# Four-wave fillers in the second attention, and sums of gelu outputs by accumulating DMAs

## The chip, the cores and the metric

The kernel runs on one core of one Trainium2 chip. The metric is device time in microseconds (us) of one execution. Three executions of the kernel before took 3659.13 us in the median (3658.23 to 3659.21).

The engines are named as in the profile: PE multiplies matrices, PEld loads its weights, DVE (vector engine) and ACT (scalar engine) work element by element and read PSUM, POOL (GpSimd) does small vector work and issues DMAs, and SP issues DMAs.

## The reference

The input x is 16 images of 256 channels by 32x32 pixels, so 1024 tokens of 256 channels for each image. Two layers follow one another, all in float32:

```
# layer 0: attention with 4 heads of 64, residual added to the tokens
qkv  = xs @ w_proj + b_proj
attn = softmax(q k^T * 64**-0.5);  res = (attn v) @ w_out + b_out + xs

# layer 1: group norm, attention with 8 heads of 32, then an MLP
x = x + attention(group_norm(x), qkv_w, proj_w, proj_b, phys_bias)
h = group_norm(x)
h = gelu(mlp_w1 h + mlp_b1)          # 256 -> 1024 channels
x = x + (mlp_w2 h + mlp_b2)          # 1024 -> 256 channels
```

## The kernel before

**Batches and stages.** The 16 images (batches b = 0 to 15) are a software pipeline. One pass of the loop runs attention_0 of batch b (L0's heads of 64, function `attention_a`), then the first half of the MLP of batch b-1 (`hidden`), then the q and k of layer 1 for batch b, then attention_1 of batch b (`attention_b`). Beside attention_1, PE also does the second half of the MLP of batch b-1 (`outputs`) and the q, k and v of layer 0 for batch b+1 (`first`): these are the fillers.

**attention_b.** Its work is cut into 16 units of two key blocks each, plus a last step, here called steps 0 to 16. In step n, PE computes the scores of unit n (`s_b`, L563, 32 matmul records), then the weighted values of unit n-1 (`acc_b`, L607, 16 records, always in PSUM bank 0), and then the fillers of this step. ACT takes the exponentials of the scores (`e_b`, L578). DVE sums the exponentials (`es_b`, L591) and adds the weighted values to the result (`res_b`, L620), or ACT copies them in steps 1, 5, 9 and 13 (L618). The first scores of the next step go to banks 0 and 1 and the rest to "wide" tiles. There are three wide tiles of two banks each, taken in turn, the one used longest ago first; a filler also takes a wide tile, unless a number in `aside` sends it to bank 0 or 1. A tile can be written again when its reader is done: so the scores of step n+1 wait for the L620 of step n and for the copies of its fillers.

**Denominators.** For b = 1 to 14, when a group of four units is complete, its summed exponentials are folded from 128 to 64 partitions by two DMAs (`fold`, L632 and L633): SP copies one half to `packed_b`, and POOL adds the other half with an accumulating DMA. Three ticks later PE sums the result (`den_b`, L642); the inverse then travels through DMAs of SP to `rd_b` and is multiplied in by DVE (L682).

**Fillers.** A q or k piece of layer 0 (`first[0]` to `first[7]`) is 16 records of 512 columns. A v piece, of layer 0 (`first[8]` to `first[11]`) or of layer 1 (`v[0]` to `v[3]`), is 32 records of 256 columns in 32-column form. An output piece (`reduce`) is 32 records of 512 columns. The list `fill` says after which step each one runs. In batches 1 to 14 the q and k of layer 1 come just before step 0 by `qk_by_seven`, 14 pieces in a chain of seven products for each half, and one v piece stands before the last of them. `weigh` of unit n needs `v[n]` (n = 0 to 3).

**The MLP by seven products.** Both halves of the MLP use seven products of half size in place of eight. In `mlp`, the 16 tiles of gelu outputs `gs` (128x512) are combined by sums and differences before the second half's products read them: first in `finish` (the call of `combine` with one index, minus), and later in `reduce`, where a product with a `then` entry calls `combine(*then, True)` for four tiles (L1112). The list `products` gives the order and the three `then` entries: after product 2, (0,0) += (1,1); after 3, (0,1) += (0,0); after 4, (1,0) += (0,0). Product 1 reads (0,0) after that, product 6 reads (0,1), product 7 reads (1,0). A product with two destinations copies its PSUM tile to `lent` on ACT, and its additions (L1171, and `then`) run one tick later.

**What sets the order.** The program is written as one stream. A planner puts it into one queue for each engine: it walks through a simulated time and gives an engine, among the instructions that are ready, the one that was written first. An instruction that is not ready yet is overtaken. `keep_in_program_order` ties an instruction behind the one written before it on its engine, as `add` does with all sums of exponentials but the first of a unit. `Later` holds callbacks that run after a number of ticks; a tick is run in every step before the fillers. At run time each engine executes its queue strictly in order, and waits on semaphores.

Of the kernel before, what the change touches and what calls it, by code (L numbers as in the profile page):

```python
# [11 lines left out]
ALU = mybir.AluOpType  # L12
# [247 lines left out]
def first_pass(ctx, tc, x, out, k):  # L260
    nc = tc.nc
    B, C, S = x.shape
# [25 lines left out]
    def load_blocks(m, b, at_end=False):  # L288
        if not at_end:
            t = act.tile([P, 7, TB], F32, tag="ws", name=f"w{m}_{b}")  # L290
            nc.sync.dma_start(t, kept_blocks[m])
            blocks[m] = [t[:, n] for n in range(7)]
            return
        one = act.tile([P, 4, TB], F32, tag="k0", name=f"w{m}_{b}_0")
        two = act.tile([P, 4, TB], F32, tag="x", name=f"w{m}_{b}_1", bufs=3)
        nc.sync.dma_start(one, kept_blocks[m][:, :4])
        nc.sync.dma_start(two[:, :3], kept_blocks[m][:, 4:])
        blocks[m] = [one[:, n] for n in range(4)] + [two[:, n] for n in range(3)]
# [11 lines left out]
    def wide(name, n=None):  # L310
        if n is None:
            n = next(m for m in order if m not in kept)
        use(n)
        return ps_s.tile([P, 2, TB], F32, tag=f"s{n}", name=name)

    def bank(name, n):
        return ps_a.tile([P, TB], F32, tag=f"b{n}", name=name)
# [12 lines left out]
    def load_x(b):  # L330
        t = act.tile([P, CC, S], F32, tag="x", name=f"x_{b}", bufs=3)
        n = S if b else TB
        for s0 in range(0, S, n):
            for cc in range(CC):
                nc.sync.dma_start(
                    t[:, cc, s0 : s0 + n], x[b, cc * P : (cc + 1) * P, s0 : s0 + n]
                )
        return t
# [15 lines left out]
    def product(o, w, r, **flags):  # L354
        for c0 in range(0, P, cols[0]):
            sl = slice(c0, c0 + cols[0])
            nc.tensor.matmul(o[sl], w[:, sl], r, **flags)  # L357
# [681 lines left out]
    def mlp(b, xb):  # L1039
        n4 = HC // 2  # L1040
        gs, open_sums = {}, {}
# [67 lines left out]
        def combine(to, what, plus, only=None):  # L1109
            for i in range(n4) if only is None else (only,):  # L1110
                d = gs[(*to, i)]
                (nc.vector.tensor_add if plus else nc.vector.tensor_sub)(  # L1112
                    d, d, gs[(*what, i)]
                )
# [17 lines left out]
        def reduce(number, right, outs, then):  # L1132
            ps = wide(f"m2_{b}_{number}")[:, 0, :]
            for i in range(n4):
                product(
                    ps, blocks[2][number - 1][:, i * P : (i + 1) * P], gs[(*right, i)],
                    start=(i == 0), stop=(i == n4 - 1),
                )
            bias, num = None, 1
            if len(outs) == 1:  # L1140
                bias = k["m2b2"]

                num = 2 if b == B - 1 and number == 7 else 1
            elif number in (2, 5):
                bias = k["m2b"]
            co = outs[0][0]
            if len(outs) == 2:

                if not lent:
                    lent.append(act.tile([P, 4, TB], F32, tag="v0", name=f"lent_{b}"))  # L1150
                m = lent[0][:, number % 4]
                if bias is not None:
                    nc.scalar.activation(m, ps, AF.Identity, bias=bias[:, co : co + 1])
                    bias = None
                else:
                    nc.scalar.copy(m, ps)
                ps = m

            def add_up():
                for co, t, plus in outs:  # L1160
                    missing[co, t] -= 1
                    n = TB // num
                    for u in range(num):
                        sl = slice(t * TB + u * n, t * TB + (u + 1) * n)
                        y, p = xb[:, co, sl], ps[:, u * n : (u + 1) * n]
                        if bias is not None:
                            nc.vector.scalar_tensor_tensor(
                                y, p, bias[:, co : co + 1], y, ALU.add, ALU.add
                            )
                        else:  # L1170
                            (nc.vector.tensor_add if plus else nc.vector.tensor_sub)(y, y, p)  # L1171
                        if not missing[co, t]:
                            nc.sync.dma_start(out[b, co * P : (co + 1) * P, sl], y)
                if then:
                    combine(*then, True)


            if len(outs) == 2 and b < B - 1:
                later.after(1, add_up)
            else:  # L1180
                add_up()
# [13 lines left out]
    def run_pieces(pieces, tick=True):  # L1195
        for piece in pieces:
            piece()
            if tick:
                later.tick()
# [14 lines left out]
    ps, n = bank("bqk", 0), brow.shape[0]  # L1214
# [10 lines left out]
    for m in (1, 2):  # L1225
        made = act.tile([P, 7, TB], F32, tag="ws", name=f"w{m}_made")
# [23 lines left out]
    for b in range(B):  # L1250
        def load_next(b=b):
            if not b:
                xs[1] = load_x(1)
                return
            with tc.issue_after(spread_out["last"].ins):
                load_blocks(1, b - 1)
                if b + 1 < B:
                    xs[b + 1] = load_x(b + 1)

        later.after(14, load_next)  # L1260
        xn = []
        seven = 0 < b < B - 1
        load_qk, sums_for_qk, qk_pieces = qk_by_seven(b)
        run(
            attention_0(
                b, tiles0, xs[b],
                lambda st, b=b, xn=xn, seven=seven, then=sums_for_qk: group_norm(
                    f"g{b}", xs[b], st, k["g1w"], k["g1b"], "res", xn, 2 if b else 3,
                    then if seven else None,
                ),  # L1270
            )
        )
        if seven:
            load_qk()
        first = []
        if b + 1 < B:
            tiles0, (first_qk, first_v) = qkv_0(b + 1, xs[b + 1])
            first = first_qk + first_v
        run_pieces(first if b == 0 else hidden)
        later.flush()  # L1280
        if b:
            load_blocks(2, b - 1)
        if b == B - 1:
            load_blocks(1, b, True)
        tiles1, (qk, v) = qkv_1(b, xn[0])
        n = len(qk) // CC

        if seven:  # L1290
            made = qk_pieces(*tiles1[:2])
            run_pieces(made[:-1] + v[:1] + made[-1:])
        else:
            aside.extend((1, 0))
            run_pieces(qk[:n] + v[:1])
        def early(piece):
            aside.append(0)
            piece()

        own = [lambda: early(v[1]), qk[n], v[2], qk[n + 1], v[3], *qk[n + 2 :]]  # L1300
        now, end = outputs, []
        if b == 0:
            first = []
        if b == B - 1:

            now, end = outputs[:3], outputs[3:]
        if not first:

            fill = {m: [piece] for m, piece in enumerate(own[:5:2] + own[1::2] + own[6:])}
            fill.update({len(own) + 3 * m: [piece] for m, piece in enumerate(now)})  # L1310
            now = []

        if first:
            o = [[piece] for piece in now]
            f = [first[1:2]] + [first[n : n + 2] for n in range(2, 10, 2)]
            fill = dict(enumerate((
                [own[0], v[2]], [v[3], first[0]],
                o[0], f[0], o[1], o[2], f[1], o[3], f[2], o[4], f[3], o[5], f[4], o[6],
                [], first[10:11],
            )))  # L1320
            fill[last + 1] = first[-1:]
        hn = []
        run(
            attention_1(
                b, tiles1, xs[b],
                lambda st, b=b, hn=hn: group_norm(
                    f"h{b}", xs[b], st, k["g2w"], k["g2b"], "q1", hn,
                    *((3 if b + 1 < B else 1), lambda y, b=b: sums_of_input(b, y)),
                ),
            ),  # L1330
            fill,
        )
        run_pieces(end)
        hidden, outputs = mlp(b, xs[b])
# [309 lines left out]
```

## Time and profile before

| | |
|---|---|
| time, median of 3 | 3659.13 us |
| time of the profiled execution | 3658.71 us |
| span of the profile | 3656.9 us |
| PE busy | 3620.8 us (99%) |
| DVE busy | 2739.4 us (75%) |
| ACT busy | 2140.2 us (59%) |
| POOL busy | 198.6 us (5%) |
| granted PE clock | 0.999 |
| DMA by POOL (queue q0) | 28.21 MB, 5.0% of the 16 DMA engines' span |

The span is what the profile covers; the execution's own time is 1.8 us longer. A busy share belongs to the whole span: PE at 99% says that PE has nearly always a matmul in it, not that it runs at its peak, since a matmul that waits behind another one counts as busy. So the profile is best read by steps: how long from one step's first score matmul to the next one's, and what that step had to do. In a timeline, the columns are start, duration, engine, line, operation, and in brackets the idle time of that engine before it and what ended it.

### The profile page before, as it was taken

The page shows a single profiled execution, that of the slowest core. Times are in us where ns is not written, and L with a number is a line of the kernel's source. Part 1 is how long each engine was busy: PE and PEld are TensorE (multiplying, and loading weights), DVE is VectorE, ACT ScalarE, POOL GpSimd, SP SyncE. Part 2 cuts the span into 40 slices and gives each one's busy share as a digit, 9 for nine tenths or more (in the row PEclk, how much of TensorE's full clock was granted, in tenths as well). Part 3 has the DMA queues.
Part 4 walks back from the last instruction along what each step waited for, and adds up shares of the span by engine and source line. Part 5 has one row for each costly group of instructions (what it writes and reads, how often), then busy time and mean ns, then how long its engine had stood idle before and what let it go on. Part 6 is the DMA issues. An engine that isn't in the chain of part 4 may idle for free.

```text
span 3656.9 us, 79215 instructions
## 1 busy us (share of the span) xinstructions
PE 3620.8 (99%) x33829; PEld 1352.0 (37%) x33829; DVE 2739.4 (75%) x3560; ACT 2140.2 (59%) x2861; POOL 198.6 (5%) x317
## 2 busy tenths in 40 slices
PE   9999999999999999999999999999999999999998
PEld 3433343333433334333343433434334343333433
DVE  5687777777777777877778777787777877777787
ACT  4665656556565655656556565565655656556572
POOL 4000000000000000000000000000000000000000
PEclk9999999999999999999999999999999999999999
DMA  3011211212121121211312112121221212203100
GB/s 122 10 54 38 58 60 38 66 41 75 41 47 57 41 77 39 51 59 36 77 39 54 56 46 67 39 54 56 53 60 39 54 56 53 66 33 63 52 26 26
DMA packets 81566, 190.28 MB, mean 52 GB/s; under 512 B 37974, under 2 KB 38742, under 8 KB 76982
## 3 DMA queue, kind: packets, MB, share of 16 engines
q1 hardware_dynamic: 71828, 156.53, 14.0%
q0 software_dynamic: 7632, 28.21, 5.0%
q8 instruction: 267, 4.37, 0.5%
q14 instruction: 93, 0.76, 0.1%
q10 hardware_dynamic: 1746, 0.40, 0.1%
HBM read 118.51 MB, written 21.75 MB: 38 GB/s over the span
## 4 chain that ended last, share of the span: by engine, by line
PE 82%; issue 10%; DVE 7%; ACT 1%; DMA 1%; POOL 0%; SPq 0%; ACTq 0%; DVEq 0%; POOLq 0%
PE s_b L563 13%; PE s_a L425 12%; PE acc_a L446 12%; PE acc_b L607 11%; PE m L357 9%; PE qk_a L357 5%; PE qk L972 3%; PE v_a L357 3%; PE v_b L357 3%; PE j L357 3%; PE m L1050 2%; PE o L357 2%; DVE es_b L591 2%; PE qk7y L972 1%; PE den_a L479 1%
## 5 line engine op out<-in xcount | busy, mean ns | idle before, releaser
L578 ACT ACTIVATE e_b<-s_b 128x1024 f32<-128x1024 f32 (+1 forms) x1280 | 982.6, 865 | 237.8 <-PE s_b L563 237.8
L591 DVE TENSOR_TENSOR es_b<-es_b,e_b 128x1024 f32<-128x1024 f32 x768 | 899.2, 1219 | 199.6 <-ACT e_b L578 198.3
L433 ACT ACTIVATE e_a<-s_a 128x1024 f32<-128x1024 f32 x512 | 520.8, 1024 | 360.2 <-PE s_a L425 343.6
L563 PE MATMUL s_b<-q,k 32*64 32x512 f32 x8192 | 543.4, 601 | 13.0 <-DVE res_b L620 10.7
L425 PE MATMUL s_a<-q,k 64*64 64x512 f32 x4096 | 544.3, 593 | 0.0
L446 PE MATMUL acc_a<-e_a,v 64*64 64x512 f32 x4096 | 540.1, 589 | 0.0
L460 DVE TENSOR_TENSOR es_a<-es_a,e_a 128x1024 f32<-128x1024 f32 x384 | 473.3, 1233 | 67.5 <-ACT e_a L433 48.0
L607 PE MATMUL acc_b<-e_b,v 128*32 128x512 f32 x4096 | 492.1, 598 | 0.0
L357 PE MATMUL m<-g,w 128*32 128x512 f32 (+1 forms) x3320 | 404.3, 592 | 0.0
L563 PEld LDWEIGHTS s_b<-q,k 32*64 32x64 f32 x8192 | 170.2, 130 | 359.9 <-issue 150.3
L446 PEld LDWEIGHTS acc_a<-e_a,v 64*64 64x64 f32 x4096 | 187.9, 133 | 251.5 <-issue 222.9
L425 PEld LDWEIGHTS s_a<-q,k 64*64 64x64 f32 x4096 | 175.9, 133 | 246.7 <-issue 212.6
L1050 PE MATMUL m<-gn_h,w 128*128 128x512 f32 x512 | 243.7, 604 | 6.0 <-DVE g L1076 3.4
L357 PE MATMUL qk_a<-x,wp 128*32 128x512 f32 (+1 forms) x1856 | 235.3, 593 | 3.7 <-ACT k L834 3.7
L607 PEld LDWEIGHTS acc_b<-e_b,v 128*32 128x32 f32 x4096 | 108.5, 109 | 351.5 <-ACT e_b L578 194.7
L357 PEld LDWEIGHTS m<-g,w 128*32 128x32 f32 (+1 forms) x3320 | 121.4, 112 | 262.3 <-issue 230.6
L1112 DVE TENSOR_TENSOR g<-g,g 128x512 f32<-128x512 f32 x320 | 206.7, 678 | 8.7 <-ACT g L1063 8.5
L620 DVE TENSOR_TENSOR res_b<-res_b,acc_b 128x512 f32<-128x512 f32 x192 | 130.7, 681 | 102.1 <-PE acc_b L607 102.1
L591 DVE TENSOR_TENSOR es_b<-e_b,e_b 128x1024 f32<-128x1024 f32 x128 | 150.7, 1218 | 64.4 <-ACT e_b L578 64.4
L1050 PE MATMUL m<-hs,w 128*128 128x512 f32 x384 | 177.9, 592 | 0.1
L460 DVE TENSOR_TENSOR es_a<-e_a,e_a 128x1024 f32<-128x1024 f32 x64 | 78.4, 1225 | 108.0 <-ACT e_a L433 107.9
L1063 ACT ACTIVATE g<-g,m1b 128x512 f32<-128x512 f32 x128 | 92.2, 723 | 109.1 <-DVE g L1092 82.1
(179 smaller groups left out, 3092.9 us busy)
## 6 DMA issues: line engine op xcount, KB each, us to landing
w<-w_kept SPq DMA_DIRECT2D x30, 1792.0 KB
packed_b<-es_b SPq DMA_DIRECT2D x42, 512.0 KB
packed_b<-es_b POOLq DMA_DIRECT2D x42, 512.0 KB, 6.5
d_a<-row_a SPq DMA_DIRECT2D x64, 256.0 KB
rd_b<-row_b SPq DMA_DIRECT2D x252, 64.0 KB
out_dram<-x SPq DMA_DIRECT2D x63, 256.0 KB
x<-in_x_dram SPq DMA_DIRECT2D x30, 512.0 KB
qk<-qk_kept SPq DMA_DIRECT2D x14, 512.0 KB
```

The lines of the kernel that those rows point to most:

```text
L357: nc.tensor.matmul(o[sl], w[:, sl], r, **flags)
L425: nc.tensor.matmul(s[h : h + HALF, g, :], kT[g * D : (g + 1) * D, c, kb * P + h : kb * P + h + HALF], qT[g * D : (g + 1) * D, c, t * TB : ...
L433: nc.scalar.activation(e, s, AF.Exp, scale=float(D) ** -0.5)
L446: nc.tensor.matmul(accs[i][h][g * D : (g + 1) * D, :], v[h * HALF : (h + 1) * HALF, kb, c * 2 + g], e[h * HALF : (h + 1) * HALF, g, :], st ...
L460: nc.vector.tensor_add(sums[i], held[i] if kb == 1 else sums[i], e)
L563: nc.tensor.matmul(outs[g][h : h + HALF, :], kT[g * D : (g + 1) * D, c, k0 : k0 + HALF], qT[g * D : (g + 1) * D, c, t * TB : (t + 1) * TB] ...
L578: nc.scalar.activation(to, s, AF.Exp, scale=float(D) ** -0.5)
L591: ins = nc.vector.tensor_add(d, es[n % 2] if kb == 0 else d, es[n])
L607: nc.tensor.matmul(acc[g * D : (g + 1) * D, :], v[:, kb + m, c * G + g], es[2 * m + g // 2][:, g % 2, :], start=(m == 0), stop=(m == 1),)
L972: nc.tensor.matmul(to, w, st[x], start=first, stop=True, skip_group_check=not first)
L1050: nc.tensor.matmul(ps, blocks[1][number - 1][:, i * P : (i + 1) * P], inputs[b][number], start=first, stop=True, skip_group_check=not first,)
L1112: (nc.vector.tensor_add if plus else nc.vector.tensor_sub)(d, d, gs[(*what, i)])
```

## The change

There are three edits.

1. In `reduce`, for all batches but the last, the later sums of gelu outputs are no longer DVE additions. For each of the four tiles POOL issues a DMA from one SBUF tile to the other with an accumulating add. The differences in `finish` stay on DVE, and the last batch keeps DVE for all.
2. Before attention_1 (batches 1 to 14), `v[0]` no longer stands before the last piece of the q and k chain; the chain runs without it. `v[0]` and `v[1]` are the fillers of step 0, `v[2]` and `v[3]` those of step 1.
3. The other fillers are dealt anew. Before, step 1 had `v[3]` and `first[0]`, step 3 had `first[1]` alone, and steps 6, 8, 10 and 12 had two pieces of `first` each. After, steps 3, 5, 7 and 9 have two each, step 12 has `first[8]` alone and step 15 has `first[9]` and `first[10]`. The output pieces move with them: before they were in steps 2, 4, 5, 7, 9, 11 and 13, after in 2, 4, 6, 8, 10, 11 and 13.

```diff
                         if not missing[co, t]:
                             nc.sync.dma_start(out[b, co * P : (co + 1) * P, sl], y)
-                if then:
+                if then and b < B - 1:
+                    for i in range(n4):
+                        to, what = (gs[(*g, i)] for g in then)
+                        nc.gpsimd.dma_start(to, what, accum_op=ALU.add)
+                elif then:
                     combine(*then, True)
...
         if seven:
             made = qk_pieces(*tiles1[:2])
-            run_pieces(made[:-1] + v[:1] + made[-1:])
+            run_pieces(made)
         else:
             aside.extend((1, 0))
             run_pieces(qk[:n] + v[:1])
...
         if first:
             o = [[piece] for piece in now]
-            f = [first[1:2]] + [first[n : n + 2] for n in range(2, 10, 2)]
+            f = [first[n : n + 2] for n in range(0, 8, 2)]
             fill = dict(enumerate((
-                [own[0], v[2]], [v[3], first[0]],
-                o[0], f[0], o[1], o[2], f[1], o[3], f[2], o[4], f[3], o[5], f[4], o[6],
-                [], first[10:11],
+                [v[0], own[0]], v[2:],
+                o[0], f[0], o[1], f[1], o[2], f[2], o[3], f[3], o[4], o[5], first[8:9], o[6],
+                [], first[9:11],
             )))
             fill[last + 1] = first[-1:]
```

`own[0]` is `early(v[1])`: `v[1]` with its PSUM tile in bank 0.

## The prediction

> **What bounds the kernel now.** I read the page first, then the waits, then the timeline of one attention_1 (batch 8, scores from 1905.46 us on) engine by engine. The page says who is full and what the replaced additions cost.
>
> ```profile
> PE 3620.8 (99%) x33829; PEld 1352.0 (37%) x33829; DVE 2739.4 (75%) x3560; ACT 2140.2 (59%) x2861; POOL 198.6 (5%) x317
> L1112 DVE TENSOR_TENSOR g<-g,g 128x512 f32<-128x512 f32 x320 | 206.7, 678 | 8.7 <-ACT g L1063 8.5
> ```
>
> PE is the bound, and it does the same matmuls before and after, so only time in which PE waits can be won. The 180 additions that leave DVE (12 for each of 15 batches) are 122 us of DVE time, and DVE time is worth nothing unless PE waits for it. The list of waits has one such row:
>
> ```profile
> PE s_b L563 <- DVE res_b L620: 10.7, 16, 0.9
> ```
>
> Sixteen waits, about one for each batch. The timeline of steps 2 to 4 shows where:
>
> ```profile
> 1925.34 1.97 PE L563 MATMUL s_b<-q,k 32*64 32x512 f32 x32
> 1926.06 0.68 DVE L1112 TENSOR_TENSOR g<-g,g 128x512 f32<-128x512 f32 x1
> 1928.47 1.22 DVE L591 TENSOR_TENSOR es_b<-es_b,e_b 128x1024 f32<-128x1024 f32 x1
> 1928.99 1.90 PE L357 MATMUL qk_a<-x,wp 128*32 128x512 f32 x16
> 1929.60 1.29 DVE L1112 TENSOR_TENSOR g<-g,g 128x512 f32<-128x512 f32 x2
> 1930.81 0.68 DVE L620 TENSOR_TENSOR res_b<-res_b,acc_b 128x512 f32<-128x512 f32 x1
> 1931.55 1.98 PE L563 MATMUL s_b<-q,k 32*64 32x512 f32 x32 [0.66 <-DVE res_b L620]
> ```
>
> Step 3 has a short filler (one q/k piece), and DVE is still at the four additions when the accumulator in bank 0 is ready at 1929; L620 comes at 1930.81, and the scores of step 4 wait for it. Step 3 takes 6.21 us. A step with two q/k pieces takes 7.19 us (step 8, 1960.75 to 1967.94), and a second piece is 1.72 us (3.55 for two less 1.83 for one), so step 3 should take 5.47: it loses 0.74 us.
>
> **The change part by part**, for one of the batches 1 to 14.
>
> *v[0] leaves the q/k chain.*
>
> ```profile
> 1901.82 1.12 PE L972 MATMUL qk<-gn_g,qk 128*128 128x512 f32 x2
> 1901.94 0.69 DVE L1002 TENSOR_TENSOR q<-qk7p,qk 128x512 f32<-128x512 f32 x1 [0.17 <-PE qk L972]
> 1902.78 1.89 PE L357 MATMUL v_b<-wq,gn_g 128*128 128x256 f32 x8
> 1904.51 1.02 PE L972 MATMUL qk<-gn_g,qk 128*128 128x512 f32 x2
> ```
>
> The piece takes 1.73 us (1902.78 to 1904.51), and hid the DVE addition that the last product must wait for. That addition ends at 1902.63, and PE is busy with the product before it until 1902.78, so the cover is not needed: -1.73. If the last product must wait for more, it is at most one such addition, +0.69.
>
> *Step 0* keeps two v pieces (v[0], v[1] for v[1], v[2]; 5.49 us): 0 on PE. What changes is the eviction: n = 0 is copied by DVE, not ACT, and the sums of exponentials of unit 0 are tied behind that copy. PE ends the piece at 1910.95; the copy of 0.69 us can start about 0.2 later (1904.71 after 1904.51) and end at 1911.84. ACT's copy of the same place ended at 1911.67 and cost nothing. In step 14 a tile that was released 0.93 us after the scores began cost 0.12; here it would be 0.89, so +0.05, between 0 and +0.7 (where the copy stands behind a DVE addition instead). The two sums start 2.2 us later; DVE is idle 2.57 us before step 2's sum, which takes that up.
>
> *Step 1*: two v pieces (3.59 us in step 0) for a v and a q/k piece (3.56): +0.03.
>
> *Step 3*: two q/k pieces, 7.19 for 6.21: +0.98. Without the additions DVE reaches L620 when bank 0 is ready, 0.25 us after the weighted values end, as in step 4 (1935.44), and three sums of 3.49 us follow. The 1.72 us of q/k work moved here is thus paid with 0.98: the stall of 0.74 goes.
>
> *Steps 5 to 10* swap outputs and q/k pieces of equal length (3.55 each): 0.
>
> *Steps 12 and 15*: one v piece moves from 12 to 15, -1.73 and +1.73. Step 12 becomes short, so I look for a new stall there.
>
> ```profile
> 1989.94 2.68 PE L563 MATMUL s_b<-q,k 32*64 32x512 f32 x32
> 1990.82 0.66 DVE L1167 SCALAR_TENSOR_TENSOR x<-m,m2b,x 128x512 f32<-128x512 f32 x1
> 1994.29 3.64 PE L357 MATMUL v_a<-wp,x 128*32 128x256 f32 x64
> 1994.54 0.69 DVE L620 TENSOR_TENSOR res_b<-res_b,acc_b 128x512 f32<-128x512 f32 x1 [3.06 <-PE acc_b L607]
> ```
>
> DVE is idle 3.06 us before L620 here and done with it at 1995.2; the shorter step lets the next scores start at 1996.1: no stall. The inverse denominators of L682 in step 13 come by DMAs issued until 2000.8, and in the last step such a row is multiplied in 1.7 us after its last issue, so they land by 2002.5; L682 would now stand at 2002.9: 0, at most +0.5. The first line also shows a loss that stays: 2.68 us for scores that take 1.97 elsewhere, since the output product's tile is released by L1167, which stands behind three sums of exponentials. No replaced addition is near it. The same holds for step 15 (2.91 us, released by L722).
>
> *The accumulating DMAs.* POOL and queue q0 carry one of this kind already, the fold.
>
> ```profile
> 1939.85 0.95 POOL L633 DMA_DIRECT2D packed_b<-es_b  x1 [52.60 <-PE s_b L563]
> ...
> 1949.57 0.62 PE L642 MATMUL den_b<-packed_b,folded 128*32 128x128 f32 x16
> ```
>
> And the answer on that line alone gives its issue time (min, median, max in ns) and its landing:
>
> ```profile
> L633 POOL DMA_DIRECT2D packed_b<-es_b x42: 918/933/1022, 359.9 to 3351.5; - x42
> ...
> DMA to landing us min/median/max: 6.1/6.5/8.1
> ```
>
> A set of four costs POOL 4 x 0.93 = 3.7 us, three sets 11 us in a batch; POOL is idle nearly all of this stage. Nothing shows a 256 KB accumulating DMA: one takes no more than the fold's 6.5 us for 512 KB, and if four ran one after another a set would take 26 us. From start to start POOL's issue spacing and half of the bytes suggest 10 to 12 us for a set; I take 12. Who waits: product 1 for the first set, product 6 for the second, product 7 for the third. The sets are released at the start of steps 3, 7 and 9 (after products 2, 3 and 4), and those products stand in steps 10, 11 and 13, so at least 4 steps of about 7.2 us, 28 us with the shorter step 12, lie between, above even 26: 0. Queued behind them on POOL stand additions into dsum and isum, which nobody on PE awaits, and the fold. The fold's sum lands about 1946.4 and is read at 1949.57, 3 us of slack in item 0 (its step 3 set is issued 10 us earlier) and 5.8 us in item 1. Cost 0, up to +5.5 in item 1 if the third set gets ahead of the fold on q0. SP's queue gets nothing new, and its packets share the 16 DMA engines, which q0 now holds 8% of the span longer (47 MB by the page's 28.21 MB for 5.0%).
>
> The row shows 0.92 to 1.02 us for POOL's issue in a stage in which DVE is busy most of the time. A rule speaks against this edit: the Trainium skill, page "SBUF — State Buffer", summary of rules for kernel authors, says not to hide a DMA issued from GpSimd under DVE work but to use the hardware path, since descriptors can't be written while DVE holds the shared port. By it each issue might wait for one DVE operation, which would add 12 times at most 1.2 us (estimate with this trace's longest sum), 15 us to POOL and still 0 to PE; by the row, 0.
>
> **The sum.** -1.73 + 0.05 + 0.03 + 0.98 + 0 + 0 = -0.67 us for each of 14 batches: -9.4. In batch 15, which keeps its fillers, DVE drops the same additions: step 8 waits 0.65 us for L620 behind them (3532.82), and 2.57 us of them stand in the chain to the last group norm at 3588.5 to 3591, of which PE idles 0.65: I take -1.5 of 0 to -3. Together -10.9. Against the profiled execution's 3658.71 this is 3647.8; the median stands 0.4 above it, so 3648.2.
>
> **The rivals.** A measurement of this kernel can tell about 0.2% (7.3 us) from no change.
>
> *Slower: v[0] is put on PE before v[1].* In step 0, v[0]'s wide tile is released by the third exponential, 2.25 us after ACT starts (1906.58), so at 1908.8; PE would be ready at 1907.36: 1.5 us in each batch, 21 us in all, 3669. It decides if PE's queue follows the written order. Against it: v[1] is ready first (bank 0, first exponential), and the queue does leave the written order (in the chain, the sixth products of both halves stand side by side, which are not written so).
>
> *Slower: the fold gets stuck.* If the third set is issued before the fold of item 1, den_b waits 5.5 us in 14 batches: +77, about 3725. It decides if SP's copy for that fold lands after product 4 ends: in the trace POOL waits for it until 1966.48, and product 4 would end 1.5 us later. Close, but the copy is the earlier.
>
> *No change: the gain is given back* by v[0]'s copy (+0.7) or the last product (+0.69) at their upper ends: +0.6 to +1.3 in each batch, 3656 to 3666. For it speaks that both margins are within 0.2 us.
>
> *More: the stalls of steps 12 and 15 go too*, 0.71 + 0.94 us in 14 batches, 3625. Against it: both stand behind sums of exponentials, not behind the additions.
>
> **How the numbers follow.** My forecast 0.62, v[0] first 0.11, fold stuck 0.07, given back 0.15, more 0.05. Faster by over 0.2%: the forecast and "more", less a little of the forecast that ends short, 0.64. Same: most of "given back" and that little, 0.17. Slower: 0.19. The forecast's own range is 3644 to 3652. The range that leaves out the stuck fold and "more" is 3642 to 3669.
>
> **What would show it.** The wait of s_b for L620 falls from 16 rows to few; step 3 takes 7.19 us with two q/k pieces; the q/k chain runs without a v piece or idle PE; the period of a batch falls from 225.7 us (scores of batch 8 to batch 9, 1905.46 to 2131.18) to about 225.0; L1112 has 140 instructions, and POOL 180 more DMAs; no PE or PEld wait for a DMA. A PE wait for v, for qk or for packed_b would make me wrong.

## The result and the profile after

The kernel after takes 3691.88 us in the median (3688.76 to 3692.72), beside 3658.76 us for the kernel before: ratio 1.0089, 95% interval 1.0072 to 1.0107. It is slower by about 33 us. The forecast was 3648.2 us and the range ended at 3669. The profiled execution took 3692.72 us, with a span of 3690.6 us (before 3656.9), at a granted PE clock of 0.998.

The page of the kernel after: PE is still the bound, with 23.2 us more of "busy" and 33.7 us more of span. DVE lost 98 us and POOL gained 143 us, as the edit says. PE has 336 records more (34165 beside 33829), though it does the same products: in the chain of q and k, `v[0]` was 8 records of 128 columns, as the line L357 shown in the prediction has it, and as a filler it is 32 of 32 columns, 24 more in each of 14 batches. The second line is DVE's wait for the rows of the inverse denominators before L682; before it was 27.6 us.

```profile
PE 3644.0 (99%) x34165; PEld 1349.6 (37%) x34165; DVE 2641.1 (72%) x3380; ACT 2143.3 (58%) x2861; POOL 341.8 (9%) x497
L682 DVE TENSOR_TENSOR res_b<-res_b,rd_b 128x512 f32<-128x512 f32 x64 | 44.2, 690 | 135.3 <-DMA rd_b<-row_b 135.2
```

The groups by line: the additions of gelu outputs on DVE fell from 320 to 140.

```profile
L1112 DVE TENSOR_TENSOR g<-g,g 128x512 f32<-128x512 f32 x140 | 92.2, 682 | 8.7 <-ACT g L1063 8.5
```

The waits of PE (what waited, on whom, us in total, times, longest). The row that the prediction rested on, 16 waits for L620, is down to one. But two rows of PE were not there before, one of them at the top:

```profile
PE v_b L357 <- ACT e_b L578: 16.8, 14, 1.2
...
PE s_b L563 <- DVE x L1167: 2.6, 6, 0.8
...
PE s_b L563 <- DVE res_b L620: 0.9, 1, 0.9
```

The steps say how much each part moved. The table has the mean length in us over batches 1 to 14 of each step (from its first score matmul to the next step's), and the median of the stretch from step 15 to the next batch's first scores. Steps that are not listed are the same in both, to 0.01.

| | step 0 | step 1 | step 3 | step 12 | step 14 | step 15 to next batch |
|---|---|---|---|---|---|---|
| before | 5.49 | 7.20 | 6.20 | 7.92 | 7.74 | 118.40 |
| after | 6.77 | 7.98 | 7.19 | 6.28 | 8.59 | 118.41 |
| predicted for after | 5.54 | 7.23 | 7.19 | 6.19 | 7.74 | 118.40 |

So steps 0, 1 and 14 cost 1.28 + 0.78 + 0.85 = 2.91 us more in a batch, where the prediction had 0.08, and 2.83 x 14 = 40 us is nearly all of the 43.7 us between forecast and result. Step 3 and the stretch to the next batch came out as predicted (one v piece left the chain of q and k, -1.73, and one came to step 15, +1.73), and step 12 within 0.1.

**Steps 0 and 1.** First the kernel before, batch 8, where v[1] stands first and v[2] second. The two pieces (x64) start 1.90 us after the first scores, without a wait, and the copy of v[1] ends at 1910.89, before the scores of step 1 start:

```profile
1907.36 3.66 PE L357 MATMUL v_b<-wq,gn_g 128*32 128x256 f32 x64
1910.26 0.63 ACT L851 COPY v<-v_b 128x512 f32<-128x512 f32 x1
1910.95 1.97 PE L563 MATMUL s_b<-q,k 32*64 32x512 f32 x32
```

And the kernel after, batch 8 (first scores at 1925.21):

```profile
1925.21 1.97 PE L563 MATMUL s_b<-q,k 32*64 32x512 f32 x32
1926.33 3.83 ACT L578 ACTIVATE e_b<-s_b 128x512 f32<-128x512 f32 x5 [0.43 <-PE s_b L563]
1928.38 3.66 PE L357 MATMUL v_b<-wq,gn_g 128*32 128x256 f32 x64 [1.20 <-ACT e_b L578]
1931.98 2.74 PE L563 MATMUL s_b<-q,k 32*64 32x512 f32 x32
1932.11 0.59 ACT L851 COPY v<-v_b 128x512 f32<-128x512 f32 x1 [1.95 <-PE v_b L357]
1932.75 0.27 PEld L563 LDWEIGHTS s_b<-q,k 32*64 32x64 f32 x16 [0.59 <-ACT v L851]
```

PE's queue keeps the written order, v[0] and then v[1]. v[0] goes to a wide tile, which the third exponential releases, so PE idles 1.20 us; v[1], whose bank 0 was free long before, stands behind it. And so v[1] ends late: its copy on ACT runs from 1932.11 to 1932.70, and the scores of step 1, which need bank 0, wait for it (2.74 us for scores that take 1.97). The Trainium skill, "TensorE: Matmul & The Clock Gate", "Step-by-step: what each phase is for", says that the engine pulls only weight loads ahead and that matmuls stay in program order; these rows agree, as 1.20 us of idle PE were not filled with v[1], which was free to run.

**Steps 12 to 14.** Before, L682 of step 13 did not wait, and the scores of step 14 took 2.09 us (batch 8):

```profile
2004.64 0.68 DVE L682 TENSOR_TENSOR res_b<-res_b,rd_b 128x512 f32<-128x512 f32 x1
2005.05 2.09 PE L563 MATMUL s_b<-q,k 32*64 32x512 f32 x32
```

After, step 12 is shorter by 1.64 us, nearly the 1.73 that was planned, and L682 of step 13 comes that much earlier:

```profile
2017.08 1.91 PE L357 MATMUL v_a<-wp,x 128*32 128x256 f32 x32
2019.47 4.00 SPq L400 DMA_DIRECT2D rd_b<-row_b  x4
2026.11 2.78 PE L563 MATMUL s_b<-q,k 32*64 32x512 f32 x32
2026.39 0.69 DVE L682 TENSOR_TENSOR res_b<-res_b,rd_b 128x512 f32<-128x512 f32 x1 [0.60 <-DMA rd_b<-row_b]
2027.00 0.74 DVE L1167 SCALAR_TENSOR_TENSOR x<-m,m2b,x 128x512 f32<-128x512 f32 x1
```

SP issues the rows of the inverse denominators until 2023.47; they are all there at 2026.39, 2.9 us later. L682 waits for them, L1167 stands behind L682 on DVE, and L1167 is what releases the output product's tile to the scores of step 14: 2.78 us of scores, and a step of 8.43 us in this batch (7.84 to 9.51 over the batches).

**The predicted parts that came true.** Steps 3 and 4: DVE is idle for 0.43 us until bank 0 is ready, L620 starts 0.25 us after PE has gone on to the filler, and the scores of the next step take their 1.97 us.

```profile
1949.05 1.92 PE L607 MATMUL acc_b<-e_b,v 128*32 128x512 f32 x16
1950.79 3.62 PE L357 MATMUL qk_a<-x,wp 128*32 128x512 f32 x32
1951.04 0.69 DVE L620 TENSOR_TENSOR res_b<-res_b,acc_b 128x512 f32<-128x512 f32 x1 [0.43 <-PE acc_b L607]
1954.34 1.97 PE L563 MATMUL s_b<-q,k 32*64 32x512 f32 x32
```

The chain of q and k runs without the v piece: the DVE addition ends at 1923.24, and the last products, which need it, start at 1923.30:

```profile
1921.49 1.88 PE L972 MATMUL qk<-qk7t,qk 128*128 128x512 f32 x4
1922.55 0.69 DVE L1002 TENSOR_TENSOR q<-qk7p,qk 128x512 f32<-128x512 f32 x1
1923.30 1.98 PE L972 MATMUL qk<-gn_g,qk 128*128 128x512 f32 x4
```

The accumulating DMAs, by the answer on their line alone (issue time on POOL in ns, minimum, median and maximum, and landing):

```profile
L1177 POOL DMA_DIRECT2D g<-g x180: 852/1006/2322, 345.7 to 3615.6; - x180
...
DMA to landing us min/median/max: 3.3/5.2/12.3
```

No wait of PE is on them, and the fold is not stuck: `den_b` stands in steps 6, 10 and 14 as before, and steps 6 and 10 have the same 7.63 us in both kernels.

### The profile page after: what moved, and what is told of

The parts are those of the page before. It is cut to its first block, busy times and chain, and to the rows that moved or that the text cites. A ratio compares the mean times of both kernels' runs of the same rounds, so it can differ in the third digit from the quotient of the medians.

```text
span 3690.6 us, 80337 instructions
## 1 busy us (share of the span) xinstructions
PE 3644.0 (99%) x34165; PEld 1349.6 (37%) x34165; DVE 2641.1 (72%) x3380; ACT 2143.3 (58%) x2861; POOL 341.8 (9%) x497
## 4 chain that ended last, share of the span: by engine, by line
PE 76%; issue 8%; DVE 4%; ACT 1%; DMA 1%; SPq 1%; POOL 0%; DVEq 0%; POOLq 0%; ACTq 0%
PE s_b L563 12%; PE acc_b L607 11%; PE s_a L425 11%; PE acc_a L446 10%; PE m L357 9%; PE qk_a L357 5%; PE qk L972 3%; PE v_b L357 3%; PE j L357 3%; PE v_a L357 2%; PE m L1050 2%; PE o L357 1%; ACT e_b L578 1%; PE qk7y L972 1%; DMA rd_b<-row_b 1%
## 5 line engine op out<-in xcount | busy, mean ns | idle before, releaser
L563 PE MATMUL s_b<-q,k 32*64 32x512 f32 x8192 | 565.3, 601 | 5.6 <-DVE x L1167 2.6
L357 PE MATMUL m<-g,w 128*32 128x512 f32 (+1 forms) x3320 | 404.3, 592 | 0.0
L620 DVE TENSOR_TENSOR res_b<-res_b,acc_b 128x512 f32<-128x512 f32 x192 | 131.9, 687 | 209.2 <-PE acc_b L607 208.9
L357 PE MATMUL qk_a<-x,wp 128*32 128x512 f32 (+1 forms) x1856 | 234.1, 594 | 4.2 <-ACT k L834 4.2
L1177 POOL DMA_DIRECT2D g<-g x180 | 165.4, 1225 | 716.7 <-ACT e_b L578 483.1
L357 PEld LDWEIGHTS m<-g,w 128*32 128x32 f32 (+1 forms) x3320 | 120.9, 112 | 245.6 <-issue 222.2
L682 DVE TENSOR_TENSOR res_b<-res_b,rd_b 128x512 f32<-128x512 f32 x64 | 44.2, 690 | 135.3 <-DMA rd_b<-row_b 135.2
```

The costliest lines, as they stand in the source:

```text
L563: nc.tensor.matmul(outs[g][h : h + HALF, :], kT[g * D : (g + 1) * D, c, k0 : k0 + HALF], qT[g * D : (g + 1) * D, c, t * TB : (t + 1) * TB] ...
L1177: nc.gpsimd.dma_start(to, what, accum_op=ALU.add)
```

## The experiments

Two theories go into them. **T1, the order in step 0**: v[0] before v[1] makes the 1.28 + 0.78 us of steps 0 and 1; against it, that these stalls come with v[0]'s new place or its copy on DVE, whatever the order. **T2, the short step 12**: it brings L682 to rows that have not landed; against it, that the rows are late because the added DMAs are in their way. And a question is left from the prediction: which part of the change is worth anything.

The steps of all kernels, in us as in the table above, with the median time and the ratio to runs of the kernel before on the same chip (3660.0 us with the first four, 3660.4 with the next four, 3660.2 with the last two). The kernel after was measured beside 3658.8 us, so a difference from its 3691.9 us has up to 1.6 us of this in it:

| kernel | 0 | 1 | 3 | 12 | 14 | 15 to next | time | ratio (95%) |
|---|---|---|---|---|---|---|---|---|
| v[1] first | 5.49 | 7.21 | 7.19 | 6.21 | 8.73 | 118.41 | 3662.6 | 1.0007 (0.9998-1.0017) |
| two fillers in step 12 | 6.77 | 7.98 | 7.19 | 7.96 | 7.74 | 116.66 | 3680.4 | 1.0054 (1.0037-1.0071) |
| both repairs | 5.49 | 7.21 | 7.19 | 7.93 | 7.74 | 116.66 | 3650.2 | 0.9973 (0.9963-0.9983) |
| before + DMAs only | 5.49 | 7.20 | 5.47 | 7.91 | 7.74 | 118.39 | 3649.8 | 0.9970 (0.9959-0.9982) |
| after, no DMAs | 6.77 | 7.98 | 7.19 | 6.19 | 8.67 | 118.41 | 3692.1 | 1.0089 (1.0072-1.0106) |
| both repairs, no DMAs | 5.49 | 7.21 | 7.19 | 7.91 | 7.75 | 116.67 | 3651.0 | 0.9974 (0.9964-0.9984) |
| before, exchanged | 6.77 | 7.97 | 6.20 | 7.92 | 7.74 | 118.39 | 3689.1 | 1.0081 (1.0064-1.0098) |
| both repairs, 6 and 7 by ACT | 5.49 | 7.21 | 7.19 | 7.21 | 13.03 | 116.71 | 3707.6 | 1.0126 (1.0109-1.0143) |
| both repairs, 6 by ACT | 5.49 | 7.21 | 7.19 | 7.21 | 7.88 | 116.66 | 3640.6 | 0.9945 (0.9931-0.9958) |
| the same, no DMAs | 5.49 | 7.21 | 7.19 | 7.21 | 7.87 | 116.67 | 3642.2 | 0.9952 (0.9938-0.9965) |

**v[1] first.**

```diff
-                [v[0], own[0]], v[2:],
+                [own[0], v[0]], v[2:],
```

> The kernel after, with one edit: the list of step 0 is own[0], v[0] in place of v[0], own[0], so that v[1]'s piece stands first on PE, as before the change. Theory (the order is at fault): v[0]'s matmuls no longer wait for the wide tile of the third exponential (1.20 us in batch 8) and step 1's scores no longer wait for bank 0 (0.59 us), so steps 0 and 1 go back from 6.77 and 7.98 us to about 5.5 and 7.2 us: 14 x (1.28 + 0.78) = 28.8 us less than after, about 3663 us. Rival (the stalls come with v[0]'s place behind the scores at all, or with its copy on DVE, whatever stands first): steps 0 and 1 stay near 6.8 and 8.0 us and the time stays at 3692 us; between the two, if only the wait for the wide tile moves to the second place, step 0 stays long and step 1 alone gives back 0.78 x 14 = 11 us, 3681 us.

Measured: 3662.6 us, 29.3 us less than after; steps 0 and 1 at 5.49 and 7.21. The timeline of batch 8:

```profile
1909.60 1.97 PE L563 MATMUL s_b<-q,k 32*64 32x512 f32 x32
1910.72 3.83 ACT L578 ACTIVATE e_b<-s_b 128x512 f32<-128x512 f32 x5 [0.43 <-PE s_b L563]
1911.50 3.66 PE L357 MATMUL v_b<-wq,gn_g 128*32 128x256 f32 x64
1914.40 0.63 ACT L851 COPY v<-v_b 128x512 f32<-128x512 f32 x1
1915.09 1.97 PE L563 MATMUL s_b<-q,k 32*64 32x512 f32 x32
```

The pieces start where the scores end, without a wait; v[1] is copied at 1914.40, as soon as ACT is through its exponentials, and bank 0 is free at 1915.03, in time for the scores. The same two pieces with the same two copies cost 2.05 us less in this order. T1 holds, and v[0]'s place behind the scores and its copy on DVE cost 0.01.

**The kernel before, exchanged.** The counterpart: the order alone, without the change, and with another v piece in the wide tile.

```diff
-                [own[0], v[2]], [v[3], first[0]],
+                [v[2], own[0]], [v[3], first[0]],
```

> The kernel before, with only the two pieces of step 0 exchanged: v[2], own[0] in place of own[0], v[2]; v[0] stays in the chain of q and k, and there are no added DMAs. Theory (a piece in the wide tiles that stands first behind the first scores waits for the third exponential, and bank 0's piece then comes out too late for step 1): steps 0 and 1 go from 5.49 and 7.20 us to about 6.8 and 8.0 us, 14 x 2.06 = 28.8 us more, about 3689 us. Rival (the stalls belong to v[0] behind the scores): within 3 us of before, about 3660 us.

Measured: 3689.1 us, where 3689 was expected. The list of waits gets the very row of the kernel after:

```profile
PE v_b L357 <- ACT e_b L578: 16.8, 14, 1.2
```

**Two fillers in step 12.** The kernel after, with this part of the list as before the change:

```diff
-                ... o[4], o[5], first[8:9], o[6],
-                [], first[9:11],
+                ... o[4], o[5], first[8:10], o[6],
+                [], first[10:11],
```

> The kernel after, with one edit: step 12 has fillers 8 and 9 and step 15 has filler 10 alone, as before the change. Theory (the shortened step 12 brings L682 of step 13 to rows of the reciprocal that have not landed): step 12 goes back from 6.28 to about 7.9 us, step 14 from 8.59 to about 7.74 us, and step 15 is shorter by the 1.73 us of the filler: net -0.85 + 1.64 - 1.73 = -0.94 a batch, 13 us less than after, about 3679 us. Rival (the rows land later because of the added DMAs, wherever the filler stands): step 14 stays near 8.6 us, and the time stays within 3 us of 3692 us.

Measured: 3680.4 us, 11.5 less than after. Step 14 is 7.74 in every batch, step 12 is 7.96. In batch 8 L682 does not wait any more, and the scores of step 14 take 2.08 us in place of 2.78:

```profile
2020.26 0.68 DVE L682 TENSOR_TENSOR res_b<-res_b,rd_b 128x512 f32<-128x512 f32 x1
2020.66 2.08 PE L563 MATMUL s_b<-q,k 32*64 32x512 f32 x32
2020.86 0.74 DVE L1167 SCALAR_TENSOR_TENSOR x<-m,m2b,x 128x512 f32<-128x512 f32 x1
```

All added DMAs are still there, so with step 12 at its old length their traffic does not make step 14 longer.

**After, no DMAs.** The other half of that question: the short step 12 without the traffic.

```diff
-                if then and b < B - 1:
-                    for i in range(n4):
-                        to, what = (gs[(*g, i)] for g in then)
-                        nc.gpsimd.dma_start(to, what, accum_op=ALU.add)
-                elif then:
+                if then:
                     combine(*then, True)
```

> The kernel after with the combines on DVE again: no accumulating DMAs, only the fillers in fours, the single filler of step 12 and v[0] first in step 0. Theory (the order and the short step 12 alone make the loss): steps 0 and 1 stay at about 6.8 and 8.0 us, step 14 stays long, 8.1 to 8.6 us, and step 3, now with two fillers, hides DVE's lateness or keeps at most its 0.74 us: 3685 to 3702 us. Rival (the traffic of the added DMAs makes the rows of the reciprocal late): step 14 falls to 7.74 us with step 12 still at 6.2 us, so 12 us less than after or, where step 3 keeps its stall, about 3680 to 3690 us; the length of step 14 decides, not the time.

Measured: 3692.1 us, the time of after; step 14 is 8.67. L682 of batch 8 waits 0.57 us for its rows, with no added DMA in the kernel:

```profile
2023.39 2.75 PE L563 MATMUL s_b<-q,k 32*64 32x512 f32 x32
2023.64 0.69 DVE L682 TENSOR_TENSOR res_b<-res_b,rd_b 128x512 f32<-128x512 f32 x1 [0.57 <-DMA rd_b<-row_b]
2024.25 0.75 DVE L1167 SCALAR_TENSOR_TENSOR x<-m,m2b,x 128x512 f32<-128x512 f32 x1
```

T2 holds: the short step, not the traffic, makes step 14 long. Step 12 is 6.19 us in every batch here, so the 0.09 us more that it has in the kernel after came with the DMAs. The run says besides that the DMAs, one of the three edits, are worth nothing in the kernel after.

**Both repairs.** The kernel after with `[own[0], v[0]]` and `first[8:10]`, `first[10:11]`.

> Both edits: own[0] before v[0] in step 0, and fillers 8 and 9 in step 12. Theory: the chain of q and k shorter by 1.73 us, step 3 longer by 0.98 us, all other steps as before the change: -0.7 a batch against the kernel before, 14 x -0.7 = -10 us, about 3648 us, faster than before. Rival 1 (the stalls at steps 0 and 1 are not the order's): 3679 us. Rival 2 (v[0] behind the scores pushes another wait into steps 0 to 2, by 0.5 us or more): within 3 us of before, 3656 to 3662 us.

Measured: 3650.2 us, 0.9973 of before. The two repairs add up (29.3 + 11.5 = 40.8; 3691.9 - 3650.2 = 41.7), and a batch takes 224.98 us in place of 225.72: -0.74, where the prediction's sum was -0.67. No step is longer than before by more than 0.01 us but step 3, which has a piece more.

**Before + DMAs only.** The first edit of the change, alone.

> The kernel before, with only the later sums of gelu outputs by accumulating DMAs; fillers and v[0] where they were. Theory: the stall of step 3 (0.74 us in batches 1 to 14) goes, as DVE no longer has 4 combines in front of the residual sums, no other step changes: 14 x -0.74 = -10 us, about 3648 us. Rival (the added 47 MB of the copies on the queue of POOL delay the rows of the reciprocal, which L682 waits for): steps 9, 13 and 14 get longer by 0.3 to 0.9 us each, which gives back the 10 us or more: 3656 to 3670 us.

Measured: 3649.8 us; step 3 goes from 6.20 to 5.47, the length that the prediction had worked out for it without its stall. L620 of step 3 (batch 8) starts when bank 0 is ready, and the scores of step 4 take their 1.97 us:

```profile
1925.02 1.90 PE L357 MATMUL qk_a<-x,wp 128*32 128x512 f32 x16
1925.27 0.69 DVE L620 TENSOR_TENSOR res_b<-res_b,acc_b 128x512 f32<-128x512 f32 x1 [0.43 <-PE acc_b L607]
1926.85 1.97 PE L563 MATMUL s_b<-q,k 32*64 32x512 f32 x32
```

The rival's late rows are there, but in one place: the last packets of the rows for the second L682 of a batch (steps 9 and 10) end 14.6 us after their reciprocal in the mean, beside 12.1 before, and DVE waits 57.1 us for rows in all, beside 27.6. But those of step 13 are on time, no step is longer, and the first edit alone brings all that the forecast hoped of the three.

**Both repairs, no DMAs.** The other two edits alone, repaired.

> Both repairs (own[0] before v[0]; two fillers in step 12) and the combines on DVE: of the change only v[0] behind the scores and the fillers in fours are left. The kernel before has 3660.0 us and the version with both repairs and the DMAs 3650.2 us. Theory A (the two parts are two ways to the same 0.74 us of step 3: PE has 1.73 us more work there while DVE catches up): step 3 is 7.19 us, about 3650 us, and the DMAs are worth nothing beside the fillers. Theory B (the DMAs alone make the gain): step 3 is 7.9 us, about 3660 us.

Measured: 3651.0 us; the intervals of the two ratios, with and without DMAs, overlap nearly whole. DVE does the four additions in step 3 (batch 8) and reaches L620 at 1928.40, 1.6 us after bank 0 was ready, but the step now has a second piece, and the next scores start at 1930.12 without a wait:

```profile
1926.58 3.62 PE L357 MATMUL qk_a<-x,wp 128*32 128x512 f32 x32
1927.19 1.28 DVE L1112 TENSOR_TENSOR g<-g,g 128x512 f32<-128x512 f32 x2
1928.40 0.68 DVE L620 TENSOR_TENSOR res_b<-res_b,acc_b 128x512 f32<-128x512 f32 x1
1930.12 1.11 PE L563 MATMUL s_b<-q,k 32*64 32x512 f32 x16
```

Theory A holds: the DMAs and the fillers in fours are two ways to the same 0.74 us. The one takes away DVE's work before L620, the other gives PE 1.72 us more to do meanwhile. Done together they gain it once.

**Product 6 and 7 by ACT.** With both repairs a stall is left in step 12, the one that the prediction called a loss that stays. This kernel goes for it: the two products with a single destination are also copied by ACT into `lent`, so that the scores need not wait for L1167.

```diff
-            if len(outs) == 2:
+            if len(outs) == 2 or b < B - 1:
```

> The version with both repairs and the DMAs, and one thing that the change does not touch: in batches 0 to 14 ACT also copies the products 6 and 7 out of their bank (as it does products 1 to 5), and DVE adds from that copy. Theory (the 0.74 us by which step 12 is longer than its neighbours is the wait of its scores for L1167, which stands behind the sums of exponentials on DVE): step 12 goes from 7.93 to 7.19 us, 14 x 0.74 = 10 us less than 3650 us, about 3640 us, faster than both kernels. Rival (ACT is late with the copy, between exponentials of 1.0 us): step 12 keeps 0.4 us or more, 3645 us or above.

Measured: 3707.6 us. Step 12 is 7.21, as the theory says, but step 14 is 13.03. The rows of batch 8:

```profile
2033.07 0.69 ACT L1153 ACTIVATE lent<-m,m2b 128x512 f32<-128x512 f32 x1 [2.85 <-PE m L357]
2033.79 0.69 DVE L1171 TENSOR_TENSOR x<-x,lent 128x512 f32<-128x512 f32 x1 [3.32 <-ACT lent L1153]
2034.51 1.07 ACT L851 COPY v<-v_a 128x512 f32<-128x512 f32 x2 [0.76 <-DVE x L1171]
2035.15 1.57 PE L563 MATMUL s_b<-q,k 32*64 32x512 f32 x16 [0.28 <-ACT v L851]
```

The copies of the two v pieces of step 12 (L851) wait for the addition of product 7 in step 14. The code says why: `lent` is allocated under the tag of the buffer `v0`, which is where the next batch's v goes, and product 7's slot must be read before the v pieces of step 12 may be written. The copies hold the wide tiles of the scores meanwhile, and exponentials and weighted values are late behind them. PE's queue left the written order here: 16 of the 32 score records of step 13 stand behind product 7, and the 13.03 us begin with them. Steps 13 and 14 together are 20.09 us in the mean, where both repairs have 14.93.

**Product 6 by ACT.** Product 7 is left alone: in step 14 its wait for L1167 was only 0.11 us.

```diff
-            if len(outs) == 2:
+            if len(outs) == 2 or number == 6 and b < B - 1:
```

> The version with both repairs and the DMAs, and ACT copies product 6 alone out of its bank, not product 7: its slot of the lent tile lies in the buffer of the next batch's v, whose first copies stand in step 12, and so product 7 held those copies back into step 14. Theory (that buffer made the 5.3 us of step 14; the wait of step 12 for L1167 is gone as before): step 12 at 7.2 us, step 14 at 7.74 us or, where L682 comes 0.72 us earlier than the rows, up to 0.2 us more: 3640 us, at most 3643 us. Rival (the shorter step 12 brings the rows of the reciprocal into the way again, as in the kernel after): step 14 at 8.2 us or more, 3646 us or above.

Measured: 3640.6 us, 0.9945 of before (0.9931 to 0.9958): a version that beats both kernels. In step 12 of batch 8 ACT copies the product while the first scores run, which take 1.97 us and no longer 2.68:

```profile
1983.61 1.97 PE L563 MATMUL s_b<-q,k 32*64 32x512 f32 x32
1983.75 0.69 ACT L1153 ACTIVATE lent<-m,m2b 128x512 f32<-128x512 f32 x1 [2.37 <-PE m L357]
```

Step 14 is 7.88 in the mean, 0.14 more than with the long step 12, so the rows of L682 are now just at the edge. T2 gives this too: L682 is 0.72 us earlier here, not 1.64.

**The same, no DMAs.**

> The same with the combines on DVE, so without the added DMAs. Theory (the DMAs are worth nothing beside the fillers in fours): within 3 us of the run with the DMAs, about 3640 us. Rival A (the traffic delays the rows of the reciprocal, which matters once step 12 is short): step 14 is shorter here than with the DMAs, and the time is 2 to 6 us lower. Rival B (DVE's 98 us more of combines come back as waits of PE): 3645 us or above.

Measured: 3642.2 us, within the 3 us; step 14 is 7.87, so the traffic does not show here either. Neither rival is seen.

## Why the prediction was wrong

**The step that failed** is step 0: "keeps two v pieces (v[0], v[1] for v[1], v[2]; 5.49 us): 0 on PE". The two pieces cost the same, but they stand in the other order. The prediction had the mechanism as its rival "v[0] is put on PE before v[1]", with the right place and releaser, and gave it 0.11. It argued that v[1] would be ready first and the queue does leave the written order, from one example in the chain of q and k. The queue did not leave it here (it did in the kernel with products 6 and 7 copied by ACT, so neither can be taken for granted). Where the code hands over an order, the order is the case to cost, and an overtaking has to be shown; the planner's choice was the first thing to settle and was not in the profile of before.

**The rival's price was too low.** It had 1.5 us a batch for the wait on the wide tile, which measured 1.20 (and 1.28 on the step), but it did not ask what is late next: v[1], second now, leaves bank 0 late, and step 1 pays 0.78 more. Together 2.06 x 14 = 28.8 us in place of 21; the order alone cost the kernel before 28.7 us (3689.1 - 3660.4). By the rival's own case plus this, the time would be 3648.2 + 28.8 = 3677, still 15 short of the result; most of that is the next term.

**The second failed term** is L682 in step 13: "0, at most +0.5". It measured +0.85 a batch on step 14, 12 us. The term's landing time, 1.7 us after the last issue, came from another place, the rows of the last step. The rows of step 13 took 2.9 us after the end of their issue in batch 8, and L682 waited 0.60 us for them. With a margin of 0.4 us worked out from one other place, the upper end should have been taken from the spread of the same transfer: in the trace of before the rows' last packets end 11.5 to 12.9 us after the reciprocal (L384) over the batches, and L682 stood 13.99 us after it. In the trace of after L682 starts 0.5 to 1.0 us behind the last packet, so with 1.64 us less, at 12.35, it is too early for most batches.

**What was right.** The chain without v[0]: -1.74, no stall. v[0]'s copy on DVE: 0 (5.49 us with v[1] first; +0.05 predicted). Step 1 with two v pieces: +0.01 (+0.03). Step 3: 7.19, to the hundredth, and 5.47 for a step with one piece and no stall. Steps 5 to 10: 0. The accumulating DMAs: 0 on PE, the fold not stuck, no product waits for a sum. The sum over these parts, -0.67 a batch, is what both repairs give: -0.74. Batch 15 was put at -1.5 and gave -0.5 (175.87 to 175.38 us from its first scores to the end of the span): step 8 lost its 0.69 us of waiting, as the prediction said, but step 9 took 0.70 back, and step 10 is 0.33 shorter.

**What was right by number and wrong by reason.** Step 3's gain was put down to the additions that leave DVE. With the second q/k piece the stall goes without that: the runs without DMAs have the same step 3. The forecast counted the gain once, so its sum is not touched, but the first edit alone has the whole of it. And that the DMAs cost PE nothing was in part luck: the prediction weighed their own landing and the fold, and did not ask what they do to other transfers. They made rows late by several us in steps 9 and 10, where PE had other work (last section).

**The rule weighed in the prediction** did not show itself. The Trainium skill ("SBUF — State Buffer", summary of rules for kernel authors) advises against hiding a GpSimd-issued DMA under a DVE operation, and gives as the reason that its descriptors starve while DVE is in its 2x or 4x mode; the prediction left this condition out. No run here shows in which mode a DVE instruction ran. The issues took 0.85 to 2.32 us, with a median of 1.0, where the fold's took 0.92 to 1.02 before. But the 76 of the 180 issues during which DVE was busy throughout took 0.93 us in the mean, and the other 104 took 1.44, so in this trace the long ones do not go with a busier DVE; what made them long is not shown. PE paid nothing for them; the kernel before with these DMAs alone is 10 us faster.

## What to carry to other kernels

When two pieces are dealt to the same slot, cost both orders: look up which buffer each one lands in and when that buffer comes free, and put the one whose buffer is free first; the wrong order here cost 2.06 us a slot and outweighed everything that the change gained. A step that gets shorter brings everything behind it nearer to its DMAs, so compare its new place with the spread of that same transfer over all its occurrences, not with one landing time from elsewhere. And before two edits are made for one stall, try each alone: here either gave the whole 10 us and both gave it once.

## What the runs showed of the hardware beyond what was expected

The same transfer of rows, issued alike in every batch of the same program, ended 11.6 to 13.4 us after the reciprocal that starts it in the kernel after (14 batches), and step 14 ranged over 1.7 us with it. Without the added DMAs it is much the same: 11.8 to 13.1 us, and 8.0 to 9.2 us for step 14.

The accumulating DMAs of 256 KB within SBUF landed 5.2 us after the issue in the median, 12.3 at most, beside 6.6 for the fold's 512 KB. They did delay other transfers: with both repairs DVE waited 74.4 us for the rows of L682 with the DMAs and 28.3 us without. Nearly all of the difference is at the second L682 of each batch, which starts in step 10: the last packets of its rows end 16.8 us after their reciprocal with the DMAs and 12.4 without (means of 14 batches), while for the third, in step 13, it is 12.4 in both. But these are waits of DVE in steps where PE has other work, and the time is the same, 3650.2 and 3651.0 us.
